# A first stage rebuilt around three tiles: statistics on ScalarE, clamps on GpSimd, and a new order of the pools

## The chip, the cores and the metric

The kernel runs on one core of a Trainium2 chip. A core has five engines that run their own instruction streams and meet at semaphores: TensorE (PE in the profile, with its weight loads as PEld), VectorE (DVE), ScalarE (ACT), GpSimd (POOL) and SyncE (SP, which here only issues transfers). Transfers are made by 16 DMA engines, fed from queues on SP, ACT and POOL. The metric is the device time of one execution in microseconds; lower is better.

## The reference

Two graph layers over 3327 nodes with 1024 features. What the change touches is the first: a layer norm, a 4-bit quantised product with a 1024x1024 weight that is normalised by its own mean and deviation, and a product with the dense adjacency.

```python
h = jnp.maximum(_layernorm(x, axis=-1), 0.0)
# _L0_gnn_ref
w_norm = (weight - jnp.mean(weight)) / jnp.std(weight, ddof=1)
weight_q = _weight_quant(w_norm, wgt_alpha, 3)       # clip to [-1, 1], round to 7 steps
x = _act_quant(h, act_alpha, 4)                      # min with 1, round to 15 steps
support = relu(jnp.matmul(x / act_delta, weight_q / wgt_delta) * act_delta * wgt_delta)
output = jnp.matmul(adj / asf, _act_quant(support, act_alpha2, 4) / support_delta)
x = x + output * asf * support_delta
# second layer: attention over the mask adj > 0 with 8 heads, then a four-layer MLP
h = jnp.maximum(_layernorm(x, axis=-1), 0.0)
x = x + _L1_gnn_ref(h, adj, W, a1, a2, W1, b1, W2, b2, W3, b3, W4, b4)
```

## The kernel before

Nodes are padded to 26 tiles of 128 rows. The kernel has four stages one behind the other: (1) quantised support, (2) adjacency product, layer norm and the heads' features, (3) attention, (4) the MLP. A scheduler orders each engine's stream from program order and readiness; `tc.keep_in_program_order` pins an instruction to the written order of the pinned ones on its engine. Pools of tiles lie on a stack in SBUF; a buffer is taken again when the last user of its former content is done, and a transfer into it waits for that in SP's queue, with everything behind it.

*Stage one.* `load` fetches two node tiles (`fetch`, L242), takes their mean and variance on DVE (`measure`, two `bn_stats` of 512 columns and a `bn_aggr`), and makes a scale and a bias per row (`normalise`, L256, through `inverse_std`, L127: a square root on ACT, then a refinement step on DVE). `quantise` (L270) makes integers: one activation into uint8 (`xb`, L273) and a clamp at 15 on DVE (`xq`, L276). `transposed` (L279) turns the tile over on PE into PSUM and copies it back on ACT (`xqt`, L284). Tiles 0 and 1 are prepared first, while the weight arrives in eight blocks of 128 rows (L290). DVE takes the statistics of all eight blocks (L294); two tiny products with a matrix of ones spread mean and variance over the partitions (`average`, L232).

Then the weight is quantised in 16 parts of 128x512 (column half `c`, row block `k`): an affine step into int8 (`wb`; ACT at L318, DVE for every fourth part at L316) and a clamp to [-7, 7] on DVE (`w_int`, L319). The products of tiles 0 and 1 (L332, `mm`, two accumulators in PSUM) run as parts become ready. Tiles 2 and 3 are loaded behind the weight and measured within the second half. The loop over 26 tiles then loads two tiles ahead of the ones it quantises, multiplies one tile with 16 products, and evacuates it through ACT (`sb`, L366) and DVE (`s_int`, L367) into the buffers in which all of the support stays.

*Stage two* multiplies each column tile of the adjacency, split into a rounded part `hi` (ACT, L179) and a rest `lo` (DVE, L183), with the support (L443), adds x, normalises (`normalised`, L145) and forms the heads' features (`heads`), which go through DRAM to stage three. `next(columns)` in the last but one round of stage one prepares the first part; the heads' weights (`whead`, `a1_t`, `a2_t`) are loaded in stage one at tile 2.

*Stage three* multiplies selections `sel` (DVE, L617) with features `f_even` and `f_odd` (L626), interleaved with full-mask products (L534). Its loads are issued by SP around the end of stage two.

Of the kernel before, what the change touches and what calls it, by code (L numbers as in the profile page):

```python
# [8 lines left out]
F32 = mybir.dt.float32  # L9
# [10 lines left out]
P = 128  # L20
# [24 lines left out]
GT = 2  # L45
# [14 lines left out]
def two_layer_kernel(  # L60
# [44 lines left out]
    const.tile([P, 120], F32, name="gap")  # L105
# [21 lines left out]
    def inverse_std(var, n, eps, tag):  # L127

        v, s, r, q = (small.tile([P, n], F32, tag=tag + c, name=tag + c) for c in "vsrq")
        nc.vector.tensor_scalar(v, var, eps, None, ALU.add)  # L130
        nc.scalar.activation(s, v, AF.Sqrt)
        nc.vector.reciprocal(r, s)
        nc.vector.tensor_tensor(q, v, r, ALU.mult)
        nc.vector.tensor_tensor(q, q, s, ALU.add)
        nc.vector.tensor_scalar(q, q, 0.5, None, ALU.mult)
        nc.vector.reciprocal(r, q)
        return r

    def statistics(stats, src, ordered=False):
        for c in range(FC):  # L140
            ins = nc.vector.bn_stats(stats[:, c, :], src[:, c * 512 : (c + 1) * 512])
            if ordered:
                tc.keep_in_program_order(ins)

    def normalised(dst, src):  # L145
# [5 lines left out]
        r = inverse_std(mv[:, 1:2], 1, EPS, "ln")  # L151
        nc.vector.tensor_scalar(dst, src, mv[:, 0:1], r, ALU.subtract, ALU.mult)

    def normaliser(mv, n, eps, factor, tag):

        rs = inverse_std(mv[:, :, 1], n, eps, tag)
        nc.vector.tensor_scalar(rs, rs, factor, None, ALU.mult)
        nb = small.tile([P, n], F32, tag=f"{tag}n", name=f"{tag}n")
        nc.vector.scalar_tensor_tensor(nb, mv[:, :, 0], -1.0, rs, ALU.mult, ALU.mult)
        return rs, nb  # L160
# [7 lines left out]
    with tc.tile_pool(name="wh", bufs=1, reuse_waits="tile") as whp, tc.tile_pool(  # L168
        name="at", bufs=2, reuse_waits="tile"
    ) as atp, tc.tile_pool(name="mm", bufs=2, space=PSUM) as mm_ps:  # L170

        def adjacency(t, js, mk):
# [4 lines left out]
            nc.sync.dma_start(at, adj_t[t][:, r, :])  # L177
# [6 lines left out]
            nc.vector.tensor_scalar(mk[:, r], at, 0.0, None, ALU.is_gt)  # L184
# [14 lines left out]
        row = const.tile([1, 4], F32, name="row")  # L199
        for i, ap in enumerate((asf, wgt_alpha, act_alpha, act_alpha2)):  # L200
            nc.gpsimd.dma_start(row[:, i : i + 1], ap.rearrange("(o d) -> o d", o=1))
        every = const.tile([P, 4], F32, name="every")
        row_ps = mm_ps.tile([P, F], F32, tag="mm", name="row_ps")
        nc.tensor.matmul(row_ps[:, :4], ones[:1], row, start=True, stop=True)
        nc.vector.tensor_copy(every, row_ps[:, :4])
        asf_t, wa_t, aa_t, aa2_t = (every[:, i : i + 1] for i in range(4))
        r_asf = reciprocal(asf_t, "r_asf")
        r_wa = reciprocal(wa_t, "r_wa")
        r_aa = reciprocal(aa_t, "r_aa")
        r_aa2 = reciprocal(aa2_t, "r_aa2")  # L210
        act_delta = scaled(aa_t, 1.0 / QA, "act_delta")
        wgt_delta = scaled(wa_t, 1.0 / QW, "wgt_delta")
        sup_delta = scaled(aa2_t, 1.0 / QA, "sup_delta")

        to_q = scaled(r_aa, QA, "to_q")
        to_w = scaled(r_wa, QW, "to_w")

        to_s = const.tile([P, 1], F32, name="to_s")
        nc.vector.tensor_tensor(to_s, act_delta, wgt_delta, ALU.mult)
        nc.vector.tensor_scalar(to_s, to_s, r_aa2, QA, ALU.mult, ALU.mult)  # L220

        w_life = ExitStack()
        w = large(w_life, "w", [P, KF, F])


        with tc.tile_pool(name="s1", bufs=2, reuse_waits="tile") as s1, tc.tile_pool(
            name="s1_tp", bufs=2, space=PSUM, reuse_waits="tile"
        ) as tp_ps:
            w_int = s1.tile([P, KF, F], BF16, name="w_int", bufs=1)
            w_stats = s1.tile([P, KF, FC, 6], F32, name="w_stats", bufs=1)  # L230

            def average(col, tag):  # L232

                ps = mm_ps.tile([P, F], F32, tag="mm", name=f"{tag}p")
                nc.tensor.matmul(ps[:, 0:1], ones, col, start=True, stop=True)
                r = small.tile([P, 1], F32, name=tag)
                nc.vector.tensor_scalar(r, ps[:, 0:1], 1.0 / P, None, ALU.mult)
                return r
# [3 lines left out]
            def fetch(t0):  # L242
                xs = s1.tile([P, GT, F], F32, name="xs")
                mv = s1.tile([P, GT, 2], F32, name="mv")
                for q, t in enumerate(range(t0, t0 + GT)):
                    load_rows(xs[:, q], x, t)
                return xs, mv

            def measure(group, q, ordered=False):

                xs, mv = group
                stats = s1.tile([P, FC, 6], F32, name="stats1")
                statistics(stats, xs[:, q], ordered)
                nc.vector.bn_aggr(mv[:, q], stats.rearrange("p c s -> p (c s)"))

            def normalise(group, t0):  # L256

                xs, mv = group
                rs, nb = normaliser(mv, GT, EPS, to_q, "l0")
                for q in range(GT):  # L260
                    ready[t0 + q] = xs[:, q], rs[:, q : q + 1], nb[:, q : q + 1]

            def load(t0):
# [523 lines left out]
```

## Time and profile before

| what | us |
|---|---|
| median of three runs (2315.4 to 2319.2) | 2317.66 |
| the profiled execution, its own time | 2316.48 |
| its span, first to last instruction | 2314.7 |
| PE busy | 2252.5 (97%) |
| DVE busy | 1567.1 (68%) |
| ACT busy | 1003.0 (43%) |
| POOL busy | 119.0 (5%) |
| first product of stage one starts | 26.50 |
| first product of stage two starts | 146.66 |
| last product of stage two is followed by the hand-over at | 957.33 |

All times within the kernel are counted from the span's start. A row of the timeline gives start, duration, engine and line, operation, result and operands with their shape, the number of merged instructions, and in brackets the idle time before it with what ended it. A row of the windows view gives a stretch, its length and each engine's busy time in it. Matmuls overlap, so a row's duration is longer than the distance between two starts.

### The profile page before, as it was taken

What the parts mean: (1) busy time and instruction counts of PE and PEld (TensorE: products, weight loads), DVE (VectorE), ACT (ScalarE), POOL (GpSimd) and SP (SyncE); (2) the same over time, 40 slices, a digit from 0 to 9 for tenths busy, and PEclk for the clock granted to TensorE, in tenths of its full rate; (3) what the DMA queues carried; (4) which work ended last, traced back from release to release, by engine and by line L of the source; (5) the groups of instructions that cost most, each with busy time, mean ns of one, the idle gap of its engine ahead of it and who ended that gap; (6) DMA issues with size and microseconds to landing.
All of it is one profiled execution on the core that took longest, in us unless ns stands there. A gap on an engine that the chain in (4) does not pass through costs nothing. (4 is left out here: it accounts for less than half of the span.)

```text
span 2314.7 us, 32013 instructions
## 1 busy us (share of the span) xinstructions
PE 2252.5 (97%) x12884; PEld 1788.4 (77%) x12896; DVE 1567.1 (68%) x2090; ACT 1003.0 (43%) x1654; POOL 119.0 (5%) x173
## 2 busy tenths in 40 slices
PE   4999999999999999899999999999999999999999
PEld 2467777777777777589999999999999999644444
DVE  7845555555555555487999999999999999812211
ACT  4743334333333333346555555555555555311110
POOL 0000011011110110100000000000000000000000
PEclk9999999999999999999999999999999999999999
DMA  6324444444444444743324241545242332433311
GB/s 231 128 90 149 147 159 135 154 157 149 152 152 137 165 155 144 278 145 112 112 73 147 80 146 45 197 156 162 79 143 83 117 105 71 152 109 114 131 56 55
DMA packets 150302, 304.94 MB, mean 132 GB/s; under 512 B 10173, under 2 KB 91021, under 8 KB 150153
## 3 DMA queue, kind: packets, MB, share of 16 engines
q1 hardware_dynamic: 130248, 229.72, 29.7%
q0 software_dynamic: 19904, 73.17, 9.7%
q8 instruction: 101, 1.65, 0.3%
q14 instruction: 49, 0.39, 0.1%
HBM read 216.07 MB, written 86.79 MB: 131 GB/s over the span
## 5 line engine op out<-in xcount | busy, mean ns | idle before, releaser
L617 DVE SCALAR_TENSOR_TENSOR sel<-srow,ndst,mask 128x896 fp32r<-128x896 f32 (+1 forms) x832 | 869.6, 1082 | 61.2 <-PE acc L626 49.7
L534 PE MATMUL mps<-dw,mf 128*128 128x260 f32 x2704 | 462.7, 284 | 0.0
L443 PE MATMUL mm<-s_int,hi 128*128 128x512 f32 x1352 | 433.0, 399 | 0.0
L443 PE MATMUL mm<-s_int,lo 128*128 128x512 f32 x1352 | 421.6, 391 | 0.0
L626 PE MATMUL acc<-f_even,sel 128*128 128x260 f32 x2704 | 403.9, 284 | 1.4 <-DVE sel L617 1.3
L533 ACT CAST mf<-mask 128x1664 fp32r<-128x1664 uint8 x208 | 330.0, 1588 | 167.1 <-PE mps L534 129.3
L626 PE MATMUL acc<-f_odd,sel 128*128 128x260 f32 x2704 | 393.9, 285 | 6.9 <-DVE sel L617 6.8
L534 PEld LDWEIGHTS mps<-dw,mf 128*128 128x128 f32 x2704 | 379.8, 188 | 9.3 <-ACT part L538 8.4
L626 PEld LDWEIGHTS acc<-f_odd,sel 128*128 128x128 f32 x2704 | 352.6, 188 | 15.9 <-DVE sel L617 12.2
L626 PEld LDWEIGHTS acc<-f_even,sel 128*128 128x128 f32 x2704 | 356.7, 188 | 5.9 <-DVE sel L617 2.8
L443 PEld LDWEIGHTS mm<-s_int,lo 128*128 128x128 f32 x1352 | 253.8, 188 | 57.6 <-issue 5.7
L443 PEld LDWEIGHTS mm<-s_int,hi 128*128 128x128 f32 x1352 | 252.1, 188 | 55.6 <-issue 5.7
L184 DVE TENSOR_SCALAR mk<-at 128x896 uint8<-128x896 f32 x104 | 61.7, 593 | 262.6 <-DMA at<-in_adj_t 261.9
L179 ACT CAST hi<-at 128x896 fp32r<-128x896 f32 x104 | 92.7, 891 | 328.7 <-PE mm L443 294.8
L384 PE MATMUL whm<-whead,ht 128*128 128x512 f32 x416 | 186.9, 602 | 0.8 <-ACT ht L381 0.8
L731 PE MATMUL o<-weights,h 128*128 128x512 f32 x416 | 179.7, 592 | 0.0
L731 PEld LDWEIGHTS o<-weights,h 128*128 128x128 f32 x416 | 79.0, 190 | 99.1 <-issue 99.0
L384 PEld LDWEIGHTS whm<-whead,ht 128*128 128x128 f32 x416 | 77.5, 191 | 98.1 <-issue 87.7
L183 DVE TENSOR_TENSOR lo<-at,hi 128x896 fp32r<-128x896 f32 x104 | 106.6, 1025 | 51.3 <-ACT hi L179 39.9
L538 ACT COPY part<-mps 128x260 f32<-128x260 f32 x104 | 39.1, 376 | 216.3 <-PE mps L534 216.3
L741 DVE TENSOR_TENSOR yo<-o,nodes 128x1024 f32<-128x1024 f32 (+1 forms) x27 | 31.8, 1182 | 146.0 <-PE o L731 146.0
L332 PE MATMUL mm<-w_int,xqt 128*128 128x512 bf16 x404 | 98.3, 393 | 9.5 <-DVE w_int L319 7.3
(128 smaller groups left out, 1566.9 us busy)
## 6 DMA issues: line engine op xcount, KB each, us to landing
feat_d<-fw POOLq DMA_DIRECT2D x26, 1040.0 KB, 5.3
f_even<-feat_d SPq DMA_DIRECT2D x7, 3380.0 KB, 12.8
f_odd<-feat_d SPq DMA_DIRECT2D x7, 3380.0 KB, 13.6
at<-in_adj_t SPq DMA_DIRECT2D x52, 448.0 KB, 3.9
at<-in_adj_t SPq DMA_DIRECT2D x52, 384.0 KB, 3.1
mask<-mask_d SPq DMA_DIRECT2D x39, 416.0 KB, 7.7
dw<-dsum_d SPq DMA_DIRECT2D x16, 910.0 KB, 5.1
dsum_d<-dw POOLq DMA_DIRECT2D x26, 520.0 KB, 6.5
```

Of the source, the lines that this page charges most:

```text
L179: ins = nc.scalar.copy(hi, at)
L183: nc.vector.tensor_tensor(lo, at, hi.bitcast(F32), ALU.subtract)
L184: nc.vector.tensor_scalar(mk[:, r], at, 0.0, None, ALU.is_gt)
L332: nc.tensor.matmul(mm[:, c * 512 : (c + 1) * 512], xqts[t][:, k, :], w_int[:, k, c * 512 : (c + 1) * 512], start=(k == 0), stop=(k == KF - 1),
L384: nc.tensor.matmul(whm, ht[:, k, :], whead[:, k, :], start=(k == 0), stop=(k == KF - 1))
L443: nc.tensor.matmul(mm[:, c * 512 : (c + 1) * 512], which[:, q, :], s_int[j][:, c * 512 : (c + 1) * 512], start=(j == 0 and which is hi), s ...
L533: nc.scalar.copy(mf, mask[:, j : j + TH, :])
L534: nc.tensor.matmul(ps, mf[:, j % TH, :], dw[:, j, :], start=(j == 0), stop=(j == T - 1))
L538: nc.scalar.copy(part[:, i % 7], ps.rearrange("p (q c) -> p q c", q=2))
L617: nc.vector.scalar_tensor_tensor(sel[:, :nb], srow[:, :nb], ndst[:, j, h : h + 1], mask[:, :, j, :], ALU.is_gt, ALU.mult,)
L626: nc.tensor.matmul(accs[b], sel[:, b, :], f[:, j, :], start=(j == 0), stop=(j == T - 1))
L731: nc.tensor.matmul(ps[:, c * 512 : (c + 1) * 512], h3[:, k, q * P : (q + 1) * P], w4[:, k, c * 512 : (c + 1) * 512], start=(k == 0), stop= ...
```

## The change

It has these parts.

1. The four scalars are loaded from ACT's queue instead of POOL's. Tile 2 is loaded ahead of the weight and tile 3 behind it; `fetch` has three buffers.
2. Statistics: tile 2, weight block 2 and tile 3 are measured on ACT (`measure_on_scalar`: a pass that sums, two small scalings, a pass that sums the squares about the mean). DVE measures tiles 0 and 1 and the other seven blocks.
3. Clamps: `xq` of tiles 0 to 2 and the odd parts of `w_int` go to GpSimd.
4. Tiles 0, 1 and 2 are quantised and transposed ahead of the weight; tile 3 is quantised between the two column halves and transposed behind them; tiles 4 and 5 are measured within the quantisation. Each weight part feeds three products, for which PSUM has three accumulators. Instructions of this part on ACT and DVE are pinned to the written order.
5. The loop quantises and transposes four tiles ahead and loads six ahead.
6. `half_inverse` drops the final halving and, for one column, joins multiply and add; factors of 2 are put into `to_q`, `to_w` and the heads' activation.
7. The adjacency loads of column tile 0 are pinned; the heads' weights are loaded in stage two after tile 0's products; their pool, and the pool of `f_odd` in stage three, are opened later; a spacer in SBUF is 152 instead of 120 elements.

```diff
-    const.tile([P, 120], F32, name="gap")
+    const.tile([P, 152], F32, name="gap")
...
-    def inverse_std(var, n, eps, tag):
-        v, s, r, q = (small.tile([P, n], F32, tag=tag + c, name=tag + c) for c in "vsrq")
-        nc.vector.tensor_scalar(v, var, eps, None, ALU.add)
+    def half_inverse(v, n, tag):
+        s, r, q = (small.tile([P, n], F32, tag=tag + c, name=tag + c) for c in "srq")
         nc.scalar.activation(s, v, AF.Sqrt)
         nc.vector.reciprocal(r, s)
-        nc.vector.tensor_tensor(q, v, r, ALU.mult)
-        nc.vector.tensor_tensor(q, q, s, ALU.add)
-        nc.vector.tensor_scalar(q, q, 0.5, None, ALU.mult)
+        if n == 1:
+            nc.vector.scalar_tensor_tensor(q, v, r, s, ALU.mult, ALU.add)
+        else:
+            nc.vector.tensor_tensor(q, v, r, ALU.mult)
+            nc.vector.tensor_tensor(q, q, s, ALU.add)
         nc.vector.reciprocal(r, q)
         return r
...
-            nc.sync.dma_start(at, adj_t[t][:, r, :])
+            ins = nc.sync.dma_start(at, adj_t[t][:, r, :])
+            if t == 0:
+                tc.keep_in_program_order(ins)
...
-        with tc.tile_pool(name="s1", bufs=2, reuse_waits="tile") as s1, tc.tile_pool(
-            name="s1_tp", bufs=2, space=PSUM, reuse_waits="tile"
-        ) as tp_ps:
+        with tc.tile_pool(name="s1", bufs=2, reuse_waits="tile") as s1, tc.tile_pool(
+            name="s1_mm", bufs=3, space=PSUM, reuse_waits="tile"
+        ) as mm_ps, tc.tile_pool(name="s1_tp", bufs=2, space=PSUM, reuse_waits="tile") as tp_ps:
...
-            nc.gpsimd.dma_start(row[:, i : i + 1], ap.rearrange("(o d) -> o d", o=1))
+                nc.scalar.dma_start(row[:, i : i + 1], ap.rearrange("(o d) -> o d", o=1))
...
+            def measure_on_scalar(mean, squares, src, name):
+                junk = s1.tile([P, F], BF16, tag="xq", name="junk")
+                total, nmean = (s1.tile([P, 1], F32, name=name + c, bufs=1) for c in "tm")
+                pin(nc.scalar.activation(junk, src, AF.Copy, accum_out=total))
+                pin(nc.scalar.activation(nmean, total, AF.Copy, scale=-1.0 / F))
+                pin(nc.scalar.activation(mean, total, AF.Copy, scale=1.0 / F))
+                junk = s1.tile([P, F], BF16, tag="xq", name="junk")
+                pin(nc.scalar.activation(junk, src, AF.Square, bias=nmean, accum_out=squares))
...
-            load(0)
+            first, second = fetch(0), s1.tile([P, GT, F], F32, name="xs", bufs=3)
+            load_rows(second[:, 0], x, 2)
             for k in range(KF):
                 nc.sync.dma_start(w[:, k, :], w0[k * P : (k + 1) * P, :])
-            xqs = {t: quantise(t) for t in range(GT)}
-            xqts = {t: transposed(xqs.pop(t)) for t in range(GT)}
-            for k in range(KF):
-                statistics(w_stats[:, k], w[:, k, :])
+            load_rows(second[:, 1], x, 3)
...
+            weight_statistics(0)
+            xqs = {t: quantise(t, nc.gpsimd, ordered=True) for t in range(GT)}
+            weight_statistics(1)
+            normalise(second, mv2, 2, 1)
+            measure_on_scalar(w_stats[:, 0, 1:2], w_stats[:, 0, 2:3], w[:, BY_ACT], "w2")
+            xqts = {0: transposed(xqs.pop(0), ordered=True)}
+            xqs[2] = quantise(2, nc.gpsimd, ordered=True)
+            for t in (1, 2):
+                xqts[t] = transposed(xqs.pop(t), ordered=True)
+            for k in range(BY_ACT + 1, KF):
+                weight_statistics(k)
+            measure_on_scalar(mv3[:, 0, 0:1], squares[:, 1:2], second[:, 1], "x3")
...
+            between = {
+                (0, 2): lambda: normalise(second[:, 1:], mv3, 3, 1),
+                (0, 5): lambda: measure(mv4[:, 0], third[:, 0], ordered=True),
+                (1, 2): lambda: measure(mv4[:, 1], third[:, 1], ordered=True),
+                (1, 6): lambda: normalise(third, mv4, 4, GT),
+            }
             for c in range(FC):
                 r = slice(c * 512, (c + 1) * 512)
                 for k in range(KF):
-                    if c == 1 and k % 4 == 2:
-                        measure(group, k // 4, ordered=True)
-                    wb = s1.tile([P, F], I8, tag="sb", name="wb")[:, :512]
+                    wb = s1.tile([P, 512], I8, name="wb", bufs=8)
...
-                    nc.vector.tensor_scalar(w_int[:, k, r], wb, QW, -QW, ALU.min, ALU.max)
-            normalise(group, GT)
+                    if k % 2:
+                        nc.gpsimd.tensor_scalar(w_int[:, k, r], wb, QW, -QW, ALU.min, ALU.max)
+                    else:
+                        pin(nc.vector.tensor_scalar(w_int[:, k, r], wb, QW, -QW, ALU.min, ALU.max))
+                    if (c, k) in between:
+                        between[c, k]()
+                if c == 0:
+                    xqs[3] = quantise(3, ordered=True)
+            xqts[3] = transposed(xqs.pop(3), ordered=True)
...
-            mms = {t: mm_ps.tile([P, F], F32, tag="mm", name="mm") for t in range(GT)}
+            mms = {t: mm_ps.tile([P, F], F32, tag="mm", name="mm") for t in range(3)}
             for c in range(FC):
-                for t in range(GT):
-                    product(t, mms[t], c)
+                for k in range(KF):
+                    for t in range(3):
+                        product(mms[t], t, c, k)
             for t in range(T):
-                if t % GT == 0 and 0 < t < T - GT:
-                    load(t + GT)
-                if t == GT:
-                    nc.sync.dma_start(whead, w_heads.rearrange("(k p) e -> p k e", p=P))
...
+                if t % GT == 0 and t < T - 6:
+                    load(t + 6, ordered=t < 4)
...
-                if t + GT < T:
-                    xqs[t + GT] = quantise(t + GT)
-                if GT <= t + 1 < T:
-                    xqts[t + 1] = transposed(xqs.pop(t + 1))
+                if t + 4 < T:
+                    xqs[t + 4] = quantise(t + 4)
...
+                if t + 4 < T:
+                    xqts[t + 4] = transposed(xqs.pop(t + 4))
...
+                if t == 0:
+                    for dst, ap in (
+                        (whead, w_heads.rearrange("(k p) e -> p k e", p=P)),
+                        (a1_t, a1.partition_broadcast(P)),
+                        (a2_t, a2.partition_broadcast(P)),
+                    ):
+                        tc.keep_in_program_order(nc.sync.dma_start(dst, ap))
...
-    with ExitStack() as wide, tc.tile_pool(name="f1", bufs=1, reuse_waits="tile") as f1p, tc.tile_pool(
+    with ExitStack() as wide, tc.tile_pool(
...
-    ) as mdp, tc.tile_pool(name="s3", bufs=1, reuse_waits="tile") as s3, tc.tile_pool(
+    ) as mdp, tc.tile_pool(name="f1", bufs=1, reuse_waits="tile") as f1p, tc.tile_pool(name="s3", bufs=1, reuse_waits="tile") as s3, tc.tile_pool(
```

## The prediction

> **What bounds the kernel now.** I read the windows view first, cut where TensorE changes its work. Columns: stretch, length, busy time of PE, weight loads, DVE, ACT and POOL, then granted clock, DMA share and GB/s.
>
> ```profile
> 0.00:26.50 26.50, 3.80 (x23) 3.07 (x24) 18.71 (x61) 7.41 (x9) 3.07 (x11) 1.00 0.93 351
> 26.50:40.52 14.02, 10.32 (x31) 3.60 (x31) 12.03 (x32) 8.00 (x13) 0.00 (x0) 1.00 0.39 142
> 40.52:48.20 7.68, 2.04 (x17) 1.54 (x17) 6.36 (x24) 5.49 (x6) 0.00 (x0) 0.60 0.10 29
> 48.20:146.66 98.46, 94.97 (x551) 47.67 (x561) 69.95 (x190) 72.90 (x79) 0.00 (x0) 0.98 0.31 109
> 146.66:957.33 810.67, 810.67 (x3307) 597.63 (x3306) 424.64 (x698) 293.04 (x441) 81.92 (x123) 1.00 0.46 152
> 957.33:1000.00 42.67, 29.10 (x122) 17.85 (x120) 27.21 (x40) 16.27 (x26) 5.02 (x7) 0.88 0.98 336
> ```
>
> PE is full through the whole second stage, so what the first stage saves or loses arrives at 957 unchanged. The first stage has three weak stretches: start-up, a product window (26.5 to 40.5), and a hole of 7.7 us. The timeline shows the hole:
>
> ```profile
> 25.17 2.22 ACT L318 ACTIVATE wb<-w,wn,wr 128x512 int8<-128x512 f32 x3 [1.45 <-DVE wn L159]
> 26.50 7.16 PE L332 MATMUL mm<-w_int,xqt 128*128 128x512 bf16 x20 [3.58 <-DVE w_int L319]
> 40.41 2.12 ACT L366 ACTIVATE sb<-mm,to_s 128x1024 uint8<-128x1024 f32 x2 [1.21 <-PE mm L332]
> 46.06 2.17 PE L282 MATMUL tp<-ident_b,xq 128*128 128x128 bf16 x16 [5.54 <-DVE xq L276]
> 48.20 5.60 PE L332 MATMUL mm<-w_int,xqt 128*128 128x512 bf16 x16
> 116.09 0.61 PE L282 MATMUL tp<-ident_b,xq 128*128 128x128 bf16 x8
> 116.54 3.62 PE L332 MATMUL mm<-w_int,xqt 128*128 128x512 bf16 x15
> 119.99 0.61 PE L282 MATMUL tp<-ident_b,xq 128*128 128x128 bf16 x8
> ```
>
> Tiles 0 and 1 are multiplied in the window; tiles 2 and 3 are not yet normalised, so PE waits for them until 48.20. In steady state a tile costs PE 3.45 us of products (116.54 to 119.99) and 0.45 of transposes. After an idle stretch PE is slow: the weight loads of 26.5 to 31.6 and of 48.2 to 52.4 follow each other every 0.43 us, against 3.45 / 16 = 0.216 later. That cost about 10 x 0.21 = 2.1 us at 48.2. Check: 48.2 + 24 x 3.45 + 22 x 0.45 + 2.1 = 143.0; the waits printed after it (0.65, 0.55, 0.39, 1.13) make 145.7, and 0.9 us stays unexplained before 146.66.
>
> **The change, part by part.** I call W the start of the first wb activation (25.17 now).
>
> *Head up to W.* The weight's last statistics now end a DVE queue that is busy without a break from 7.87:
>
> ```profile
> 7.87 1.28 DVE L141 BATCH_NORM_STATS2 w_stats<-w 128x6 f32<-128x512 f32 x2 [0.55 <-DMA w<-in_w]
> 20.34 0.59 DVE L296 BATCH_NORM_AGGREGATE w_mv<-w_stats 128x2 f32<-128x96 f32 x1
> 23.52 0.20 ACT L131 ACTIVATE ws<-wv 128x1 f32<-128x1 f32 x1 [3.45 <-DVE wv L130]
> ```
>
> Removed from DVE: one of eight weight blocks (1.3 us) and two xq clamps (2 x 0.65); added: seven small operations for tile 2 (7 x 0.16 = 1.1). The x2 load is put ahead of the eight weight loads on SP's queue. At the 0.41 MB per us that the DMA moved between 8 and 17 us, 512 KB cost 1.28 us, so the last block lands near 17.5 and its statistics end near 19.2, about 1.1 us earlier than now. The small chain from there to W loses four operations of 0.19 (scaling merged, epsilon, multiply with add, halving): 0.8. DVE alone would give W = 25.17 - 1.1 - 0.8 = 23.3.
>
> ACT decides otherwise. Its queue is now in written order: tile 2's two passes, xb0, xb1, the weight block's two passes, xqt0, xb2, xqt1, xqt2, tile 3's two passes, and only then wb. No row has an accumulating pass; nearest are 1.00 (xqt copy) and 1.24 us (xb), so I take 1.1 and three small ones of 0.2: 2.8 us per measurement (bounds 2.4 and 5.0, the latter if accumulating doubles it). From 7.8, when x2 lands: 10.6, xb1 13.0, weight block 15.8, xqt0 16.8, xb2 18.0, then POOL's clamp (1.5, below), transposes 1.0, xqt2 21.6, tile 3 ends 24.4. If the weight's Sqrt stands behind that, 0.2 + 1.1 of chain follow and W = 25.7; ahead of it, W = 24.5. I take 25.2: the head gains nothing. Moving the four scalar loads from POOL's queue to ACT's (four issues of about 0.5 us, before ACT has work) is free; the row that waited until 9.45 arrives sooner.
>
> *POOL's clamps.* Eight of 128x512 and three of 128x1024. Nearest rows: a POOL memset of 128x1 at 0.10 us and an affine select of 128x128 at 0.28. So 0.10 + 0.18 per 128 elements: 0.82 and 1.54 us. The Trainium skill, GPSIMD Engine Reference, section 3.1, gives 1.03 to 1.8 cycles an element at 1.2 GHz for one-input bodies: 0.44 to 0.77 us for 512. I take 0.82, from the row. A rule speaks against the change: SBUF — State Buffer, "Who interferes with whom", says that DVE in its two-port modes and GpSimd exclude each other for a whole instruction. DVE's clamp of 512 elements takes 0.43 us where one element a cycle at the page's 0.96 GHz would need 0.53, so it is in such a mode. Four DVE clamps, two DVE wb and four POOL clamps per half would queue: by the rule each of the 12 DVE operations waits half a POOL clamp, 12 x 0.41 = 4.9 us on DVE; by the row alone, nothing. No run shows it yet; half of them will not overlap, and the products hide much, so I charge 0.8 below and keep 4.9 for the range.
>
> *Product window.* Products begin at W + 0.80 (wb) + 0.43 (clamp) + 0.1 = W + 1.33, as now. There are 48 instead of 32: 12 slow x 0.43 + 36 x 0.216 = 12.9. ACT needs 12 x 0.74 + xb3 1.2 = 10.1, so PE, not ACT, sets the pace. DVE carries 8 clamps (3.4), 4 wb (2.1), two measurements (3.0), xq3 (0.7) and two normalisations (2.6): 11.8 us, close behind; I add 0.8. The last product ends at W + 1.33 + 12.9 + 0.8 = W + 15.0 = 40.2, as early as now, with one tile more (3.45 us won).
>
> *The hole.* Tile 3 is transposed already. But tiles 0, 1 and 2 end together and hold all three accumulators: tile 3 must wait for sb of tile 0 (1.1) and what ACT has ahead of it (0 to 1.2), while one tile's transposes run. I take 1.5 us, against 7.7: 6.2 won. That is too short to make PE slow again, judging by the waits of 0.65 (at 62) and 1.13 us (at 104), after which the products ran at full pace: 2.1 won.
>
> *Steady part.* 23 x 3.45 + 22 x 0.45 = 89.3. The four waits and the rest (3.6 together) came from x arriving late for DVE and ACT; loads are now six tiles ahead instead of four, in three buffers. I leave 1.0 us: about 2.6 won. ACT's 3.35 us per tile (1.2 + 1.0 + 1.1) stay under 3.9; if ACT had a further 0.6, it would set the pace.
>
> Sum: end of stage one at 40.2 + 1.5 + 89.3 + 1.0 = 132.0 against 146.66: 14.6 us.
>
> *Second stage and after.* The heads' weight loads (2.5 MB) move behind tile 0's adjacency loads; first needed at tile 1's heads, a tile of 31 us later, so hidden. The pinned adjacency loads sit in SP's queue behind the last x loads, whose buffers come free four tiles (15 us) before the end: in time. One merged and one dropped DVE operation per tile are under PE, except in the last tile:
>
> ```profile
> 968.40 2.21 DVE L617 SCALAR_TENSOR_TENSOR sel<-srow,ndst,mask 128x896 fp32r<-128x896 f32 x2 [5.91 <-DMA srow<-src_d]
> 974.41 0.37 PE L398 MATMUL sp<-ident,src 128*8 128x128 f32 x1 [8.10 <-DVE lnr L136]
> ```
>
> There the chain stands behind sel, which waits for a load; two operations fewer give 2 x 0.2 = 0.4. The placing of stage three's buffers changes which release ends last (f_odd now lies on stage two's late tiles, needed only two sub-passes later); bounds -3 to +3 us, value 0. Stage three's matmuls should not care where operands lie: f_even, f_odd and dw lie apart and take 284, 285 and 284 ns.
>
> **The number.** 14.6 + 0.4 = 15.0 us. Span 2314.7 - 15.0 = 2299.7; that execution's own time, 2316.48, becomes 2301.5; the median shown is 1.18 above it: 2317.66 - 15.0 = 2302.7.
>
> **Rivals.**
> - *The feeders bind* (0.22). An accumulating pass costs 2 us (W + 2.5) and the port rule holds for most clamps (4.0 more on the window): gain 8.5, time 2309. For it: DVE's 11.8 us against PE's 12.9. Against it: three accumulators, so no clamp can hold the steady part.
> - *Everything falls into place* (0.09). Sqrt ahead of tile 3's passes and cheaper passes (W = 23.5, 1.7 more), no steady wait (1.0), the hand-over at 957 shortened by 2: gain 19.7, time 2298.
> - *The gain is given back* (0.03). SP's order at 957 puts the small srow load behind more megabytes; PE's 8.1 us wait grows by some 11 to 15 us. Time 2314 to 2318. Against it: srow's load is still issued when the last product frees its buffer.
> - *POOL is the new bound* (0.04): slower. Eight clamps in a row end the window at W + 1.6 + 8p + 0.65; this eats all 15.0 us when p passes (15.0 + 15.0 - 2.25) / 8 = 3.5 us. At p = 4.5 the time is 2326. The rows' 0.82 speaks against it.
> - The forecast: 0.62, own range 2299 to 2306.
>
> 0.2% is 4.6 us, about what a measurement of this kernel can tell from no change. Faster: 0.62 + 0.22 + 0.09 = 0.93; within it 0.03; slower 0.04. The range leaves out half of the best case, the worse quarter of the feeders' case, and the last two: 0.045 + 0.055 + 0.07 = 0.17, so 2298 to 2310.
>
> **What would show it.** W between 24.5 and 25.7 with tile 3's passes ending just before it; POOL clamps near 0.8 us; 48 products between W + 1.3 and W + 15; a gap of 1 to 2 us where 7.7 was, with no second run of 0.43 us loads; second stage beginning near 132; PE full from there. Wrong if the clamps cost over 2 us, if the first product is later than 28, or if the stretch from 957 to 1000 changes its length by more than 3 us.

## The result, and the profile after

The kernel after takes 2307.52 us (four runs, 2306.74 to 2308.5) against 2317.9 us before in the same comparison: a ratio of 0.9957, with a 95% interval of 0.9939 to 0.9974. The gain is 10.4 us where the forecast had 15.0. The profiled execution has a span of 2305.0 us (2314.7 before).

The windows view of the kernel after, cut at the same events as before (columns: stretch, length, busy time of PE, weight loads, DVE, ACT and POOL, granted clock, DMA share, GB/s):

```profile
0.00:30.98 30.98, 4.57 (x30) 3.85 (x31) 17.03 (x58) 17.02 (x32) 9.17 (x11) 1.00 0.70 271
30.98:44.82 13.84, 13.07 (x56) 5.42 (x55) 12.45 (x34) 11.65 (x17) 5.68 (x8) 1.00 0.24 76
44.82:46.27 1.45, 0.63 (x10) 0.51 (x10) 1.45 (x5) 1.45 (x3) 0.00 (x0) 1.00 0.15 28
46.27:136.67 90.40, 89.40 (x536) 44.96 (x536) 63.67 (x175) 70.51 (x77) 0.00 (x0) 1.00 0.35 119
136.67:947.52 810.85, 810.85 (x3306) 597.57 (x3305) 419.60 (x651) 293.07 (x441) 82.09 (x123) 1.00 0.47 155
947.52:978.18 30.66, 18.33 (x51) 8.84 (x50) 15.80 (x25) 10.32 (x18) 2.78 (x4) 0.83 1.01 354
978.18:2305.00 1326.82, 1311.87 (x8913) 1127.92 (x8913) 1019.18 (x1063) 606.13 (x1091) 31.43 (x35) 1.00 0.34 112
```

The hole of 7.7 us is 1.45 us, and the stretch behind it is 8 us shorter. But the first product starts at 30.98, not at 26.5: the head has become 4.5 us longer. Stage two starts 10.0 us earlier than before (136.67 against 146.66), is as long as before (810.85 against 810.67), and what follows it is too (1357.5 against 1357.4). So the whole result lies in the first stage: 4.5 us lost ahead of 31 us, some 14.5 won behind it. The miss is almost all in the 4.5 us of the head. No run undid the earlier loads of the loop, so how the 8 us behind the hole divide (a tile moved into the window, the slow restart, the waits for x) stands as the forecast summed it and is not tested.

The timeline of the kernel after shows that head (start, duration, engine, line, operation, result and operands, instructions; in brackets the idle time before and what ended it):

```profile
11.98 5.63 POOL L276 TENSOR_SCALAR xq<-xb 128x1024 bf16<-128x1024 uint8 x2 [10.54 <-ACT xb L271]
14.82 1.04 PE L282 MATMUL tp<-ident_b,xq 128*128 128x128 bf16 x8 [8.40 <-POOL xq L276]
15.94 1.06 ACT L247 ACTIVATE junk<-w 128x1024 bf16<-128x1024 f32 x1 [2.83 <-issue]
17.66 1.03 PE L282 MATMUL tp<-ident_b,xq 128*128 128x128 bf16 x8 [1.81 <-POOL xq L276]
18.81 1.15 ACT L251 ACTIVATE junk<-w,w2m 128x1024 bf16<-128x1024 f32 x1 [1.40 <-PE tp L282]
20.25 0.55 DVE L350 BATCH_NORM_AGGREGATE w_mv<-w_stats 128x2 f32<-128x87 f32 x1
22.24 2.77 POOL L276 TENSOR_SCALAR xq<-xb 128x1024 bf16<-128x1024 uint8 x1 [4.64 <-ACT xb L271]
25.06 1.04 PE L282 MATMUL tp<-ident_b,xq 128*128 128x128 bf16 x8 [6.37 <-POOL xq L276]
25.89 0.53 PE L352 MATMUL w_meanp<-w_mv,ones 128*128 128x1 f32 x2
26.14 1.01 ACT L284 COPY xqt<-tp 128x1024 bf16<-128x1024 bf16 x1 [3.15 <-PE tp L282]
26.46 0.16 DVE L354 TENSOR_SCALAR w_mean<-w_meanp 128x1 f32<-128x1 f32 x1 [5.67 <-PE w_meanp L352]
27.05 1.06 ACT L247 ACTIVATE junk<-xs 128x1024 bf16<-128x1024 f32 x1
28.52 1.15 ACT L251 ACTIVATE junk<-xs,x3m 128x1024 bf16<-128x1024 f32 x1
29.22 0.16 DVE L162 SCALAR_TENSOR_TENSOR wn<-w_mean,wr 128x1 f32<-128x1 f32 x1
29.67 0.80 ACT L381 ACTIVATE wb<-w,wn,wr 128x512 int8<-128x512 f32 x1
30.98 6.27 PE L398 MATMUL mm<-w_int,xqt 128*128 128x512 bf16 x20 [3.22 <-DVE l01v L146]
```

Read it backwards. W, the first wb, is at 29.67, and two chains end just ahead of it. The one that ends last is ACT's own queue: wb follows tile 3's two passes (27.05 and 28.52) without a wait, and these stand behind the copy of tile 2 (26.14), for which ACT waited 3.15 us. The other is the weight's scale and bias, which DVE has ready at 29.38 (wn), 0.3 us sooner: its statistics were done at 20.80 (w_mv), and it then waited 5.67 us for a tiny product on PE, the weight's mean, which runs behind tile 2's transposes. So both chains hang on these transposes (25.06). They waited for GpSimd's clamp of tile 2, which takes 2.77 us and started late, since ACT made tile 2's integers late. ACT had stood still twice (2.83 and 1.40 us) in front of its passes with the discarded output `junk`; for the first wait the profile names no releaser, and the second experiment below shows it. That output takes its buffers from the same two as `xq` (`tag="xq"`), so ACT could not write it until PE had transposed tiles 0 and 1, and these waited for GpSimd's two clamps, 5.63 us together.

That gives three suspects: the length of GpSimd's clamp, the shared buffers, and, for the second chain, the order on PE. I call this theory A. A rival, theory B, blames ScalarE itself: it has more work ahead of W (17.0 us busy in the head, 7.4 before), and W would stay late whatever happens to the three.

### The profile page after: what moved, and what is told of

Read it like the earlier page. It is cut to its first block, busy times and chain, and to the rows that moved or that the text cites. A ratio compares the mean times of both kernels' runs of the same rounds, so it can differ in the third digit from the quotient of the medians.

```text
span 2305.0 us, 31962 instructions
## 1 busy us (share of the span) xinstructions
PE 2248.7 (98%) x12896; PEld 1789.1 (78%) x12896; DVE 1549.2 (67%) x2006; ACT 1010.2 (44%) x1675; POOL 131.2 (6%) x181
## 5 line engine op out<-in xcount | busy, mean ns | idle before, releaser
L699 PEld LDWEIGHTS acc<-f_odd,sel 128*128 128x128 f32 x2704 | 353.8, 189 | 14.5 <-DVE sel L690 11.3
L187 DVE TENSOR_SCALAR mk<-at 128x896 uint8<-128x896 f32 (+1 forms) x104 | 61.5, 593 | 257.2 <-DMA at<-in_adj_t 256.6
```

Of the source, the lines that this page charges most:

```text
L187: ins = nc.vector.tensor_scalar(mk[:, r], at, 0.0, None, ALU.is_gt)
L699: nc.tensor.matmul(accs[b], sel[:, b, :], f[:, j, :], start=(j == 0), stop=(j == T - 1))
```

## The experiments

### The chain ahead of W, one link at a time

The clamps of tiles 0 and 1 go back to DVE, where they are pinned to the written order; tile 2's stays on GpSimd:

```diff
-            xqs = {t: quantise(t, nc.gpsimd, ordered=True) for t in range(GT)}
+            xqs = {t: quantise(t, nc.vector, ordered=True) for t in range(GT)}
```

> Clamps of tiles 0 and 1 back on VectorE, pinned between weight blocks 0 and 1; tile 2's stays on GpSimd; all else as after the change. Theory A (the late start W of the weight quantisation, 29.67 us, comes from a chain: slow GpSimd clamps of 2.8 us hold the buffers that ScalarE's measuring passes share with xq, so xb2 and GpSimd's third clamp are late, and PE holds the mean's product behind tile 2's transposes): the two ScalarE waits of 2.8 and 1.4 us nearly vanish, tile 2's transposes move from 25.1 to about 22.8, and ScalarE's passes over tile 3 become the last wait; W about 27.6, span about 2 us shorter. Theory B (ScalarE simply has too much to do before W; GpSimd is not at fault): W stays within 0.5 us of 29.67.

Measured: W at 27.49, stage two at 133.13, time 2303.9 us, ratio 0.9946 (0.9929 to 0.9963). W came 2.2 us earlier; of ACT's two waits 0.63 us is left. Another 1.4 us was won behind W, most of it in a shorter window and hole (13.2 and 0.9 us instead of 13.84 and 1.45); why was not followed.

The discarded output gets buffers of its own (in both passes):

```diff
-                junk = s1.tile([P, F], BF16, tag="xq", name="junk")
+                junk = s1.tile([P, F], BF16, name="junk")
```

> The discarded output of ScalarE's measuring passes gets buffers of its own instead of sharing the two xq buffers; clamps stay on GpSimd. Theory A: ScalarE measures weight block 2 at 13.0 instead of 15.9, xb2 ends near 18.1, GpSimd's third clamp near 20.9, the mean's product runs near 22.1 instead of 25.9, W about 25.8, span about 3.9 us shorter. Theory B (ScalarE's load): ScalarE has the same work, W moves by less than 1 us.

Measured: W at 25.65, stage two at 132.06, time 2302.81 us, ratio 0.9942 (0.9927 to 0.9957). The timeline of this run:

```profile
13.18 1.04 ACT L247 ACTIVATE junk<-w 128x1024 bf16<-128x1024 f32 x1
18.29 2.76 POOL L276 TENSOR_SCALAR xq<-xb 128x1024 bf16<-128x1024 uint8 x1 [0.52 <-ACT xb L271]
21.11 1.03 PE L282 MATMUL tp<-ident_b,xq 128*128 128x128 bf16 x8 [2.24 <-POOL xq L276]
21.93 0.53 PE L352 MATMUL w_meanp<-w_mv,ones 128*128 128x1 f32 x2
25.65 0.80 ACT L381 ACTIVATE wb<-w,wn,wr 128x512 int8<-128x512 f32 x1
```

Both waits of ACT are gone, the third clamp starts 4.0 us earlier although each clamp is as slow as before, and W follows by the same 4.0 us. ACT's work is unchanged, so theory B falls: its load did not hold W at 29.67. ACT's queue still ends last, at 25.65, with wn ready at 25.42.

The weight's two small products are pinned ahead of tile 2's transposes on PE, and ACT copies tile 2 behind its passes over tile 3, so the edit touches both chains:

```diff
-            for t in (1, 2):
-                xqts[t] = transposed(xqs.pop(t), ordered=True)
+            xqts[1] = transposed(xqs.pop(1), ordered=True)
...
-            nc.tensor.matmul(ps[:, 0:1], ones, w_mv[:, 0:1], start=True, stop=True)
+            pin(nc.tensor.matmul(ps[:, 0:1], ones, w_mv[:, 0:1], start=True, stop=True))
...
+            xqts[2] = transposed(xqs.pop(2), ordered=True, behind=True)
             third = fetch(2 * GT)
```

> The two small products for the weight's mean and variance are pinned on PE ahead of tile 2's transposes, and ScalarE copies tile 2 behind its passes over tile 3; nothing else. Theory A: the mean's product runs near 20.9 instead of 25.9; GpSimd's clamp still ends at 25.0, so tile 2's copy ends near 27.1 and W is about 27.1, span 2.5 us shorter. Rival (PE's order is not what holds W): W unchanged.

Measured: the mean's product at 20.54 instead of 25.89, W at 26.84, stage two at 132.44, time 2303.84 us, ratio 0.9946 (0.9931 to 0.9961). W gained 2.8 of the 5.4 us by which the mean came earlier:

```profile
25.83 1.01 ACT L286 COPY xqt<-tp 128x1024 bf16<-128x1024 bf16 x1 [0.35 <-PE tp L282]
26.84 4.33 ACT L383 ACTIVATE wb<-w,wn,wr 128x512 int8<-128x512 f32 x6
```

ACT's two waits of 2.83 and 1.40 us and GpSimd's late clamp stay in this run, and tile 2's copy still stands ahead of wb. The mean's place alone was not tried; by the trace of the kernel after, where ACT's queue ends last, it could not have brought W forward by itself.

### Why the clamp is slow

The clamp of `xq` has one operation (minimum with 15), the clamp of `w_int` has two (minimum and maximum), and the latter took 0.71 us for 512 elements. In the next kernel tiles 0 and 2 get a maximum with zero as a second operation, and tiles 1 and 2 go through int8 instead of uint8. No value changes.

```diff
-                xb = s1.tile([P, F], U8, name="xb")
+                xb = s1.tile([P, F], I8 if t in (1, 2) else U8, name="xb")
...
-                vector.tensor_scalar(xq, xb, QA, None, ALU.min)
+                if t in (0, 2):
+                    vector.tensor_scalar(xq, xb, QA, 0.0, ALU.min, ALU.max)
+                else:
+                    vector.tensor_scalar(xq, xb, QA, None, ALU.min)
```

> Three forms of GpSimd's clamp of 128x1024 into bf16 in one kernel, values unchanged: tile 0 uint8 with min and max, tile 1 int8 with min alone, tile 2 int8 with min and max. After the change uint8 with min alone takes 2.77 us, int8 128x512 with two operations 0.61 to 0.7. If the input type is what costs: tiles 1 and 2 near 1.15 us, tile 0 near 2.8. If the missing second operation is what costs: tiles 0 and 2 near 1.15, tile 1 near 2.8. If length costs more than in proportion, all near 2.8.

The GpSimd part of this run's timeline:

```profile
11.56 1.03 POOL L277 TENSOR_SCALAR xq<-xb 128x1024 bf16<-128x1024 uint8 x1 [10.12 <-ACT xb L271]
12.68 2.77 POOL L279 TENSOR_SCALAR xq<-xb 128x1024 bf16<-128x1024 int8 x1
20.08 1.04 POOL L277 TENSOR_SCALAR xq<-xb 128x1024 bf16<-128x1024 int8 x1 [4.64 <-ACT xb L271]
```

The second row is the one with a single operation: 2.77 us. With two operations it is 1.03 us, for uint8 and int8 alike. So the type does not matter and the length does not explain it; the instruction that does less takes 2.7 times as long. W was at 25.78 and the one run took 2301.88 us.

Only the second operation, for all three clamps, types as they were:

```diff
-                vector.tensor_scalar(xq, xb, QA, None, ALU.min)
+                if vector is nc.gpsimd:
+                    vector.tensor_scalar(xq, xb, QA, 0.0, ALU.min, ALU.max)
+                else:
+                    vector.tensor_scalar(xq, xb, QA, None, ALU.min)
```

> Only the three GpSimd clamps of node tiles get a second operation that changes no value (maximum with zero). Theory A: each takes 1.03 us instead of 2.77, tile 2's transposes and with them the weight's mean on TensorE come some 3 to 4 us earlier, W between 25.4 and 26.5, stage two starts at 131.8 to 133, time 2302 to 2304. Rival (the clamp's length matters little once the shared buffers hold ScalarE back): W above 28, time above 2305.5.

Measured: 2303.59 us, ratio 0.994 (0.9923 to 0.9956), stage two at 132.41. Its timeline:

```profile
12.30 2.16 POOL L277 TENSOR_SCALAR xq<-xb 128x1024 bf16<-128x1024 uint8 x2 [10.84 <-ACT xb L271]
14.51 1.06 ACT L247 ACTIVATE junk<-w 128x1024 bf16<-128x1024 f32 x1 [1.08 <-POOL xq L277]
19.40 1.04 POOL L277 TENSOR_SCALAR xq<-xb 128x1024 bf16<-128x1024 uint8 x1 [4.95 <-ACT xb L271]
21.16 0.55 DVE L353 BATCH_NORM_AGGREGATE w_mv<-w_stats 128x2 f32<-128x87 f32 x1
21.76 0.59 PE L355 MATMUL w_meanp<-w_mv,ones 128*128 128x1 f32 x2 [0.23 <-DVE w_mv L353]
25.45 0.80 ACT L384 ACTIVATE wb<-w,wn,wr 128x512 int8<-128x512 f32 x1
```

W is at 25.45. With short clamps the shared buffers cost ACT 1.1 us instead of 2.8 (the second wait is gone), and the mean's product waits for DVE's statistics, no longer for GpSimd.

Both together (two operations, buffers of its own for `junk`), with the first operation of tile 3's normalisation pinned as well:

```diff
-                junk = s1.tile([P, F], BF16, tag="xq", name="junk")
+                junk = s1.tile([P, F], BF16, name="junk")
...
-                vector.tensor_scalar(xq, xb, QA, None, ALU.min)
+                if vector is nc.gpsimd:
+                    vector.tensor_scalar(xq, xb, QA, 0.0, ALU.min, ALU.max)
...
-                (0, 2): lambda: normalise(second[:, 1:], mv3, 3, 1),
+                (0, 2): lambda: normalise(second[:, 1:], mv3, 3, 1, ordered=True),
```

> GpSimd's clamps of tiles 0 to 2 in the form with two operations (min 15, max 0, values unchanged), the discarded output of ScalarE's measuring passes in buffers of its own, tile 3's normalisation pinned behind weight part 2 on VectorE. Theory A in full: both causes of the late W are gone; third clamp ends near 19.1, tile 2's copy near 21.1, tile 3's passes near 23.8, W about 24.1, second stage near 131, span about 5.5 us shorter than after the change. If another hold stands behind (the DMA that brings the weight, or the statistics at 20.3): W between 25 and 26 as in the two runs that removed one cause.

Measured: W at 25.42, no better than either alone; 2303.2 us, ratio 0.9946 (0.9931 to 0.9961). The timeline of this run shows the next link:

```profile
15.03 6.02 DVE L337 BATCH_NORM_STATS2 w_stats<-w 128x6 f32<-128x512 f32 x10
21.19 0.55 DVE L355 BATCH_NORM_AGGREGATE w_mv<-w_stats 128x2 f32<-128x87 f32 x1
23.95 0.20 ACT L130 ACTIVATE ws<-w_var 128x1 f32<-128x1 f32 x1 [1.62 <-DVE w_var L366]
24.27 1.15 ACT L253 ACTIVATE junk<-xs,x3m 128x1024 bf16<-128x1024 f32 x1
25.42 0.80 ACT L386 ACTIVATE wb<-w,wn,wr 128x512 int8<-128x512 f32 x1
```

DVE's own statistics end at 21.05, here and in the run before it, 0.9 us later than in the kernel after: DVE's joined multiply and add for tile 2 took 0.81 us instead of 0.22 in both; why was not followed. The weight's square root stands between tile 3's two passes on ACT, so ACT waits 1.62 us for the variance and then still has the second pass ahead of the wb. So theory A in full, which had W near 24.1, does not come out: about 25.4 is where the chain through DVE's statistics ends in these two runs, with ACT's queue 0.2 us behind it. The run with `junk`'s own buffers arrives at 25.65 by the other way, through tile 2's transposes.

### The product window

All `w_int` clamps go back to DVE:

```diff
-                    if k % 2:
-                        nc.gpsimd.tensor_scalar(w_int[:, k, r], wb, QW, -QW, ALU.min, ALU.max)
-                    else:
+                    if True:
                         pin(nc.vector.tensor_scalar(w_int[:, k, r], wb, QW, -QW, ALU.min, ALU.max))
```

> All 16 clamps of w_int on VectorE, none on GpSimd; else as after the change. If the products of the window (13.84 us from the first product to the hole) run close to VectorE's pace, eight more clamps of 0.43 less 1.0 us of mutual blocking add 2.4 us to VectorE's 12.45 and the window becomes about 15.8: second stage begins near 138.7 instead of 136.67, span 2 us longer. Rival, PE sets the window (48 products at their slow and full pace, 12.9): no more than 0.5 us.

Measured: the window takes 14.6 us instead of 13.8 and stage two starts 106.3 us after the first product instead of 105.7; time 2307.99 us, ratio 0.9968 (0.9955 to 0.998), against 0.9957 for the kernel after: no difference that these intervals could tell. The window grew by 0.8 us, between the 2 us of the expectation and the 0.5 of its rival. By the trace, GpSimd's eight clamps there buy some 0.6 us, which is little against the scatter: five traces with one and the same first stage have 105.1 to 105.7 us from the first product to stage two.

Only two tiles share the weight parts, with two accumulators instead of three; the third tile is multiplied in the loop:

```diff
-            mms = {t: mm_ps.tile([P, F], F32, tag="mm", name="mm") for t in range(3)}
+            mms = {t: mm_ps.tile([P, F], F32, tag="mm", name="mm") for t in range(2)}
```

> Two accumulators and two products per weight part instead of three; tile 2 is multiplied behind the window. If feeding the window (VectorE and ScalarE at 12.45 and 11.65 us busy in it) takes about 13 us whatever PE has to do, the third tile is free in the change: here 3.45 us of products are added behind a window only 0.8 shorter, second stage near 139.3, span 2.7 us longer. Rival, PE sets the window: 16 products fewer shorten it by 3.5 us and nothing is lost.

Measured: stage two starts 109.4 us after the first product instead of 105.7; time 2311.35 us, ratio 0.998 (0.9972 to 0.9988), an interval that just touches that of the kernel after. The windows view of this run, for the window and the hole:

```profile
31.29:45.10 13.81, 11.30 (x41) 4.14 (x41) 12.42 (x36) 11.98 (x18) 5.95 (x8) 1.00 0.21 77
45.10:46.20 1.10, 0.57 (x8) 0.45 (x9) 1.10 (x4) 1.10 (x3) 0.00 (x0) 1.00 0.19 22
```

With 16 products fewer the window is as long as in the kernel after (13.81 and 13.84). So PE does not set its pace, the making of the weight parts does, and the third tile's 16 products are free there. That is worth 3.7 us. Whether a fourth tile would be free too was not tried: with three, PE is shown busy for 13.07 of the 13.84 us.

### The edits that the forecast put at nothing

The change also moved the place of tiles: the spacer grew from 120 to 152 columns, and the pool of `f_odd` is opened later. Both undone, everything else as after:

```diff
-    const.tile([P, 152], F32, name="gap")
+    const.tile([P, 120], F32, name="gap")
...
-    with ExitStack() as wide, tc.tile_pool(
+    with ExitStack() as wide, tc.tile_pool(name="f1", bufs=1, reuse_waits="tile") as f1p, tc.tile_pool(
...
-    ) as mdp, tc.tile_pool(name="f1", bufs=1, reuse_waits="tile") as f1p, tc.tile_pool(name="s3", bufs=1, reuse_waits="tile") as s3, tc.tile_pool(
+    ) as mdp, tc.tile_pool(name="s3", bufs=1, reuse_waits="tile") as s3, tc.tile_pool(
```

> Only the spacer (120 again) and the place of f_odd's pool in stage three as before the change. From the end of stage two's products to stage three's first took 31.2 us before and 30.7 after the change, from there to the end 1326.2 and 1326.8. If the placing matters, these move by 1 us or more; if not, all four stretches stay within 0.7 us of those after the change and the span within 1.

Measured: 2323.83 us, ratio 1.0035 (1.0022 to 1.0048). That is slower than before the change. Stage one was as after (stage two at 136.36), so some 18 us went in two other places, which the next two runs separate. The spacer alone:

```diff
-    const.tile([P, 152], F32, name="gap")
+    const.tile([P, 120], F32, name="gap")
```

> Only the reserved tile goes back from 152 to 120 columns (128 bytes a partition), everything allocated after it moves by that; the order of stage three's pools stays as after the change. Theory P (place sets the pace of stage two's products): stage two's 2704 matmuls run at the slow mean again (404 and 397 ns instead of 399 and 391), its products end about 12.5 us later than in the kernel after (960 instead of 947.5), the hand-over is 30 to 32 us as after, time near 2320. Rival Q (the two undone edits only act together, or the pace comes from the order of the pools): stage two ends at 947 to 948 and the time is within 2 us of 2307.5.

Measured: 2319.78 us, ratio 1.001 (1.0001 to 1.0019), span 2317.3. The groups of stage two's products in this run (columns: line, operation and shape, count, busy us, mean ns, idle before):

```profile
L509 PE MATMUL mm<-s_int,hi 128*128 128x512 f32 x1352 | 439.7, 403 | 0.0
L509 PE MATMUL mm<-s_int,lo 128*128 128x512 f32 x1352 | 427.8, 396 | 0.0
```

and in the kernel after:

```profile
L509 PE MATMUL mm<-s_int,hi 128*128 128x512 f32 x1352 | 433.0, 399 | 0.0
L509 PE MATMUL mm<-s_int,lo 128*128 128x512 f32 x1352 | 421.8, 391 | 0.0
```

The same 2704 instructions with the same operands take 12.7 us more (6.7 + 6.0), at a granted clock of 1.00, with nothing waiting. The shortest take 387 ns in both runs and the median goes from 389 to 393, so it is most of them and not a few. The weight loads are as long as before (188 ns). The hand-over keeps its 30.5 us. The order of the pools alone, with the spacer as after:

```diff
-    with ExitStack() as wide, tc.tile_pool(
+    with ExitStack() as wide, tc.tile_pool(name="f1", bufs=1, reuse_waits="tile") as f1p, tc.tile_pool(
...
-    ) as mdp, tc.tile_pool(name="f1", bufs=1, reuse_waits="tile") as f1p, tc.tile_pool(name="s3", bufs=1, reuse_waits="tile") as s3, tc.tile_pool(
+    ) as mdp, tc.tile_pool(name="s3", bufs=1, reuse_waits="tile") as s3, tc.tile_pool(
```

> Only the order of stage three's pools is undone (f_odd's pool opened first again), the reserved tile stays at 152 columns. Theory P: stage two is as after (products end at 947 to 948), but f_odd's loads stand ahead of the second source row on the DMA queue again, the hand-over is 36 to 38 us instead of 30.7, time near 2313.5. Rival Q: stage two slow as in the run with both undone, or the hand-over unchanged, time within 2 us of 2307.5.

Measured: 2313.06 us, ratio 0.9982 (0.9975 to 0.9989), span 2310.8. Stage two is as after (399 and 391 ns, its products end at 947.27), and the hand-over takes 38.6 us instead of 30.7. SP's queue in this run:

```profile
962.37 0.37 SPq L566 DMA_DIRECT2D dw<-dsum_d  x1
963.44 8.33 SPq L566 DMA_DIRECT2D f_odd<-feat_d  x2
971.88 3.30 SPq L576 DMA_DIRECT2D srow<-src_d  x1
```

and in the kernel after:

```profile
963.83 0.37 SPq L566 DMA_DIRECT2D dw<-dsum_d  x1
964.88 1.30 SPq L576 DMA_DIRECT2D srow<-src_d  x1
```

Two loads of `f_odd` stand ahead of the small source row, which is issued 7 us later; PE then waits 14.8 us for sel before its first product of stage three. The hand-over is 7.9 us longer, the span only 5.8: 1.9 us come back within stage three (1325.0 us instead of 1326.8), which was not followed. By spans the two parts add up to what both cost: 12.3 + 5.8 = 18.1, and 2323.1 - 2305.0 = 18.1.

Neither edit makes the kernel faster than it was before. The kernel before has 120 columns and the old order of the pools, and yet the fast pace (399 and 391 ns) and a hand-over of 31.2 us. So other parts of the change spoil both, and the two edits restore them; which parts do it was not tried.

One more size of the spacer tells whether 120 is an unlucky number or 152 a lucky one:

```diff
-    const.tile([P, 152], F32, name="gap")
+    const.tile([P, 184], F32, name="gap")
```

> Only the reserved tile grows from 152 to 184 columns, so all that is allocated after it moves 128 bytes a partition the other way than in the run with 120 columns. Theory P1 (the pace of stage two's products depends on the place modulo 256 bytes): slow means again (404 and 397 ns), products end near 960, time near 2320. Theory P2 (120 columns put one tile in an unlucky place, others are free): 399 and 391 ns as after, products end at 947 to 948, time within 2 us of 2307.5. A pace between or a slower one says that neither is the whole rule.

Measured: 2319.08 us, ratio 1.0014 (1.0007 to 1.002); 403 and 396 ns. A shift of 128 bytes per partition in either direction costs the same: stage two takes 823.9 us with 120 columns and 824.1 with 184, against 810.85. A period of 256 bytes fits this; three sizes do not prove it. The spacer moves all that is allocated behind it, `hi` and `lo` among it, against `s_int`, which lies at the other side; which tile's place matters was not tried.

## Why the prediction was right or wrong

- *Head, "ACT decides otherwise ... I take 25.2".* Wrong by 4.5 us: W was 29.67. That ACT's queue decides was right, and so were its order and its passes (1.06 and 1.15 us with 0.19 each for reading the sum out, against 1.1). The sum failed at two of its terms. It followed ACT's queue as if nothing else could hold it, and missed that `junk` and `xq` share a tag, so that each pass waits for transposes that wait for GpSimd: 2.83 + 1.40 us. And the clamp that tile 2's copy waits for was 2.77 us instead of 1.5. These 5.5 us cover the distance from the forecast's own 24.5, for the order in which the weight's square root stands ahead of tile 3's second pass, as it did. The weight's mean, a product on PE queued behind tile 2, was not in the sum either; as a second chain it ended 0.3 us before the first.
- *"POOL's clamps ... 0.82 and 1.54 us".* 0.71 on average and 0.61 at the least for 512 elements, where the row gave 0.82 and the page's rate 0.44 to 0.77: both held. For the clamp of 1024 with one operation 2.77 us came out, outside both: the Trainium skill, GPSIMD Engine Reference, section 3.1, gives 0.88 to 1.54 us, an estimate by its rate for one-input bodies, which only the form with two operations meets (1.03 us). The test that I wrote for it, "wrong if the clamps cost over 2 us, if the first product is later than 28", came out on the wrong side for both.
- *DVE's share of the head.* "Their statistics end near 19.2": they ended at 20.14, with w_mv done at 20.80. It cost nothing in the kernel after. In the two runs with two operations, where they ended at 21.05, they are the floor near 25.4.
- *Product window.* The end was right (W + 15.15 against W + 15.0), the reason was not. "PE, not ACT, sets the pace" is refuted by the run with two tiles. The rival "the feeders bind" was right that the feeders set the window's pace, but its two costs did not come: the passes took 1.06 and 1.15 us, not 2, and the window was only 0.15 us longer than forecast, not 4.
- *The rule of the Trainium skill, SBUF — State Buffer, "Who interferes with whom".* The timeline of the kernel after agrees with it, at a price near the 0.8 us that I charged:

```profile
36.46 1.74 POOL L383 TENSOR_SCALAR w_int<-wb 128x512 bf16<-128x512 int8 x2 [1.10 <-DVE wb L379]
36.90 1.58 DVE L385 TENSOR_SCALAR w_int<-wb 128x512 bf16<-128x512 int8 x2
```

 Two clamps side by side take 1.58 us on DVE, where two alone take 0.43 each. Over the eight of the window DVE's mean is 0.57 us, so they lost 8 x (0.57 - 0.43) = 1.1 us, not the 4.9 of the rule with full overlap. The run with all clamps on DVE is the counter-proof. Shortest, median and longest of a clamp in ns, in the kernel after and in that run:

```profile
L385 DVE TENSOR_SCALAR w_int<-wb x8: 373/427/835, 30.5 to 40.6; 128x512 bf16<-128x512 int8 x8
L383 DVE TENSOR_SCALAR w_int<-wb x16: 374/421/428, 30.8 to 44.4; 128x512 bf16<-128x512 int8 x16
```

 Without GpSimd beside it no clamp is slow.
- *The hole and the steady part.* Right: 1.45 us against 1.5, and 90.40 against 90.3, with 0.43 us loads nowhere behind it.
- *Second stage and after.* The net effect of "value 0" was right (810.85 and 30.66 us against 810.67 and 31.19), but the reasoning was not safe. "Stage three's matmuls should not care where operands lie" says nothing on stage two, whose products do: the two edits that I put at nothing hold 18 us, by which they make good what other parts of the change spoil. Without them the change would have been slower than before, which no rival of mine described. Neither half of that was in the forecast, so its value 0 was luck. The 0.4 us at the tail did not show; from the end of stage two's products to the end of the span it took 0.1 us more than before.

The sum of spans: 4.5 us of W, 0.2 of window and steady part, and 0.7 behind stage one (0.2 in stage two, 0.1 after it, and the 0.4 that did not come) make up 5.3 us of miss, 15.0 forecast and 9.7 measured.

The likeliest case's own range, 2299 to 2306, does not hold the result; the full range, 2298 to 2310, does, through the case of the binding feeders. That case had W 2.5 us and the window 4.0 us later; what came was W 4.5 us later and the window as forecast. So the number fell into the range by luck: the range reached that far for another cause of about the same size.

Four repairs of W (own buffers, two operations, both, mean first) are all near 0.994 of the time before, 3.7 to 4.7 us better than the kernel after by their medians, or 2.5 to 3.9 by their ratios. Their intervals overlap with each other and with that of the kernel after; in the traces stage two starts 4.1 to 4.6 us earlier. Which of them is the best is not settled.

## What to carry to other kernels

When work moves to another engine, sum each queue with its waits: for each output ask which buffers it takes and who must release them, even for an output that nobody reads. Where two chains end within 0.3 us of each other, as here ahead of W, look for what both hang on, since mending one alone brings next to nothing. Edits that only move a tile or reorder pools should be priced by undoing them, since they can hold more than the change that they accompany.

## What the runs showed of the hardware that was not expected

- GpSimd's tensor_scalar on 128x1024 elements of one byte, written as bf16, takes 2.77 us with one operation (minimum) and 1.03 us with two (minimum, maximum); uint8 or int8 makes no difference. Why was not tried.
- Stage two's fp32r matmuls of 128x512 take 391 and 399 ns on average, or 396 and 403 ns, depending on a shift of SBUF tiles by 128 bytes per partition: 12 to 13 us over 2704 of them, at a granted clock of 1.00 in both. Why was not shown.
